# First involution of a four-layer convolution network: which engine's queue issues the fourth copy of shifted patches

## The chip, the cores and the metric

The kernel runs on one core of one Trainium2 chip, in one launch. The metric is the device time of the whole program in microseconds (us). The kernel before took 1796.4 us, the median of three runs (1794.46 to 1797.01).

A core has five engines that run side by side, each with its own queue of instructions that it works off in order: PE (TensorE, matmuls), DVE (VectorE), ACT (ScalarE), POOL (GpSimd) and SP (SyncE, which here only issues transfers). A transfer (DMA) is issued by an instruction in the queue of SP, ACT or POOL and then runs on the core's DMA engines; its landing is told by a semaphore.

## The reference, cut to what matters

The input is x, 4 images of 256 channels of 56 x 56, all in float32. Four layers follow, each of which adds its result to x. Layers 0 and 2 are involutions, layer 1 is two 3x3 convolutions, layer 3 gates with Fourier transforms. The change touches layer 0 alone:

```python
x = x + _L0_conv_ref(_gn(x), ...)            # _gn: normalise groups of 8 channels

# _L0_conv_ref
patches = conv_general_dilated_patches(x, (7, 7), ...)      # the 49 neighbours of each pixel
patches = patches.reshape(b, G, c // G, 49, 56, 56)         # G = 16 groups of 16 channels
h = einsum('bchw,oc->bohw', x, reduce_w) + reduce_b         # 256 -> 64 channels
kern = einsum('bchw,oc->bohw', h, span_w) + span_b          # 64 -> 49 taps for each group
kern = kern.reshape(b, G, 1, 49, 56, 56)
out = (kern * patches).sum(axis=3)
```

Every pixel and group of channels has its own 7 x 7 filter, computed from the normalised input.

## The kernel before, in words

**Units and columns.** `involution_layer` works on 8 units, one for each image and each block of 128 channels. An image is cut into tiles of 3 rows by 8 columns of pixels (TY, TX); a tile needs a window of 9 x 14 = 126 pixels around it (QY, QX, Q). Seven tiles side by side make the width, so a unit has 7 columns (NTX) of 19 tiles each (NTY). There are 56 columns in the layer, numbered here from 0.

**First phase of a unit, the taps.** `tap_matrices` computes for every tile a matrix `kt` that holds the filters laid out over the window's 126 pixels. It is made of matmuls of `z_sb` with `hp` (L593), whose results DVE (L611) and ACT (L604) copy out with the bias.

**Second phase, the columns.** For each of the 7 columns the loop calls `apply`, `next_windows` and `next_strip`, in this order. `apply` multiplies the column's windows `xw` with `kt` (L635, 112 matmuls), ACT and DVE pick the right groups out of the products into `un` (L648, L655), and POOL adds them to x (L660).

**How a column's windows come about.** `next_strip` lets POOL write a normalised strip of the image, 14 pixels wide, into `strip_sb` (L391), of which there is one. `next_windows` has TensorE transpose it in seven pieces (L406), and ACT copies these into `xw` (L418). The seven pieces are the windows of every third tile, those that start on a multiple of 9 rows. The windows in between start 3 or 6 rows lower, and are put together from two neighbours: for a shift of j = 1 or 2 times 3 rows, one copy takes the lower part of a window, `xw[cut:Q]`, and one the upper part of the window after it, `xw[:cut]`, where `cut` is 42 j pixels. So there are four copies a column, all within `xw`, of 84, 42, 42 and 84 partitions with 3 KB each: 252, 126, 126 and 252 KB. The first of each pair is issued at L424, the second at L426.

**What sets the order.** `xw` has three buffers (NXW), so `next_windows` in column c makes the windows of column c + 3. For the last three columns of a unit these are the first three of the next, which are used only after that unit's taps. At a unit's start the transposes for the first call come before column 0 is applied; in the other calls they come after the column's `apply`. `in_order` keeps each engine's instructions in the order in which the program writes them. The scheduling layer adds the waits: a copy waits for ACT's L418, and the first use of `xw` in L635 waits for all four copies. SP's transfers take turns among eight semaphores, and each waits until the transfer that last used its semaphore has landed.

**What else is in these queues.** SP loads a new image's blocks at L294, in the middle of the taps. POOL also computes a power for the normalisation (L149), and stores a finished unit (L1120) after its last strip. In the last unit ACT's queue issues loads of the next layer's weights.

In layer 2 the same function runs with all four copies issued by SP; its strips are written by ACT (L389) from the third column on.

Of the kernel before, what the change touches and what calls it, by code (L numbers as in the profile page):

```python
# [35 lines left out]
Q = QY * QX  # L36
# [35 lines left out]
def net_kernel(  # L72
# [19 lines left out]
    nc = tc.nc  # L92
# [206 lines left out]
    def involution_layer(layer, xin, xout, red, span, sb, xs_of, ahead=None, pending=None):  # L299

        with ExitStack() as es:
# [91 lines left out]
            def window(ty):  # L393

                k, j = divmod(ty, TY)
                return (0, NSB, 2 * NSB - 1)[j] + k
# [3 lines left out]
            def begin_windows():  # L400

                flat = strips[len(xws)].rearrange("p h w -> p (h w)")
                ps = two_banks().rearrange("p i n -> p (i n)")
                begun_windows.append(ps)
                for k in range(NSB):
                    nc.tensor.transpose(ps[:Q, k * P : (k + 1) * P], flat[:, k * Q : (k + 1) * Q], ident_sb)  # L406

            def next_windows():

                if len(xws) == len(columns):  # L410
                    return
                if not begun_windows:
                    begin_windows()
                ps = begun_windows.pop()
                xw = work.tile([Q, NTY, P], F32, name="xw", bufs=NXW)
                xws.append(xw)

                nc.scalar.copy(xw[:, :NSB, :], ps[:Q, : NSB * P].rearrange("q (n c) -> q n c", n=NSB))  # L418

                n = NSB - 1  # L420
                for j in range(1, TY):
                    cut = TY * QX * j
                    at = window(j)
                    nc.sync.dma_start(xw[: Q - cut, at : at + n, :], xw[cut:Q, 0:n, :])  # L424
                    eng = nc.sync if layer == 2 or j == 1 else nc.gpsimd
                    eng.dma_start(xw[Q - cut : Q, at : at + n, :], xw[:cut, 1 : 1 + n, :])  # L426


            h_of = {}
# [537 lines left out]
            if layer == 0:  # L967
                place(hooks0, begin(), (1, 2, 4, 6, 7))
            else:
                since = mark()  # L970
                nc.sync.dma_start(z_sb, z2_dram)
                nc.sync.dma_start(zb_sb, zb2_dram)
                next_strip()
                run(bottleneck(0))
                hooks0[3] = list(pending[0])
                for _ in range(NXW - 1):
                    next_windows()
                    next_strip()
                hooks0[7] = [next_windows, next_strip]
            if layer == 0:  # L980
                next_strip()
                for i in range(NXW):
                    hooks0.setdefault(2 + 5 * i, []).extend((next_windows, next_strip))
# [34 lines left out]
            for u, (b, cb) in enumerate(units):  # L1018
# [24 lines left out]
                if b + 1 < B:  # L1043
                    n = 16 if layer == 0 else (26, 21)[cb]
# [714 lines left out]
```

## Time and profile before

The profiled execution is one run of the program.

| what | value |
|---|---|
| median of three runs | 1796.4 us (1794.46 to 1797.01) |
| profiled execution, first to last instruction (the page gives no other time of its own) | 1791.4 us |
| difference between the two | 5.0 us |
| first involution, layer 0 | from the start to about 513 us |
| TensorE busy, whole span | 1716.7 us (96%) |
| DVE, ACT, POOL busy | 1385.3, 813.5, 406.2 us |
| POOL's issue of the fourth copy, L426 | 56 times, 31.5 us in all, mean 563 ns |
| SP's issues of window copies between 0 and 520 us | 168 times, medians 786 (L424) and 767 ns (L426) |

In a row of the costliest groups the first part names line, engine, operation and tiles (out<-in, with partitions x elements); after the count stand busy time and the mean of one in ns, and after the second bar the idle time of the engine just ahead of such instructions, with what ended it. In the chain of waits each line has start, duration and what ran; "issue" is time in which the profile shows nothing to wait for. For waits the three numbers are the total, the number of times and the longest.

### The profile page before, as it was taken

The page shows a single profiled execution, that of the slowest core. Times are in us where ns is not written, and L with a number is a line of the kernel's source. Part 1 is how long each engine was busy: PE and PEld are TensorE (multiplying, and loading weights), DVE is VectorE, ACT ScalarE, POOL GpSimd, SP SyncE. Part 2 cuts the span into 40 slices and gives each one's busy share as a digit, 9 for nine tenths or more (in the row PEclk, how much of TensorE's full clock was granted, in tenths as well). Part 3 has the DMA queues.
Part 4 walks back from the last instruction along what each step waited for, and adds up shares of the span by engine and source line. Part 5 has one row for each costly group of instructions (what it writes and reads, how often), then busy time and mean ns, then how long its engine had stood idle before and what let it go on. Part 6 is the DMA issues. An engine that isn't in the chain of part 4 may idle for free.

```text
span 1791.4 us, 55774 instructions
## 1 busy us (share of the span) xinstructions
PE 1716.7 (96%) x24040; PEld 1507.5 (84%) x24040; DVE 1385.3 (77%) x2745; ACT 813.5 (45%) x1882; POOL 406.2 (23%) x627
## 2 busy tenths in 40 slices
PE   6999999999999999999999999999999999999998
PEld 4998988889978988898889888986888887788886
DVE  2777787767778988988898889885777778687775
ACT  2555556555533222222323132111767667567564
POOL 2224422444320000000000000001000355463572
PEclk9999999999989999999999999999999999999997
DMA  2445444633653021211111111122344567566653
GB/s 86 135 151 170 140 146 134 196 107 119 204 171 105 32 75 51 76 33 64 58 68 44 52 63 37 44 110 73 122 164 156 162 213 220 169 223 189 183 154 115
DMA packets 66003, 215.76 MB, mean 120 GB/s; under 512 B 13237, under 2 KB 20926, under 8 KB 62046
## 3 DMA queue, kind: packets, MB, share of 16 engines
q1 hardware_dynamic: 49262, 145.37, 25.9%
q0 software_dynamic: 14656, 64.77, 11.3%
q8 instruction: 190, 3.11, 0.7%
q10 hardware_dynamic: 1840, 2.05, 0.4%
q14 instruction: 55, 0.45, 0.1%
HBM read 76.30 MB, written 49.15 MB: 70 GB/s over the span
## 4 chain that ended last, share of the span: by engine, by line
PE 68%; DVE 19%; ACT 4%; DMA 4%; issue 3%; POOL 2%; SPq 1%; POOLq 0%; ACTq 0%; DVEq 0%
PE mm L1523 17%; PE ps L593 14%; PE ps L635 14%; PE mm L1441 9%; DVE kt L611 6%; PE mm L1412 5%; PE ps L406 3%; DMA xw<-xw 3%; DVE un L655 3%; PE ps L469 1%; DVE res L1516 1%; DVE xs L1375 1%; DVE st L1105 1%; ACT kt L604 1%; ACT hp L488 1%
## 5 line engine op out<-in xcount | busy, mean ns | idle before, releaser
L635 PE MATMUL ps<-kt,xw 126*32 126x48 f32 (+1 forms) x12544 | 381.8, 235 | 27.8 <-issue 12.2
L635 PEld LDWEIGHTS ps<-kt,xw 126*32 126x32 f32 (+1 forms) x12544 | 341.9, 121 | 74.5 <-issue 45.5
L593 PE MATMUL ps<-hp,z_sb 64*126 64x133 f32 x6144 | 383.2, 279 | 8.4 <-DVE kt L611 4.6
L1523 PE MATMUL mm<-v,u_sb 128*128 128x280 f32 (+1 forms) x1728 | 383.5, 383 | 1.9 <-DVE u_sb L1254 1.5
L593 PEld LDWEIGHTS ps<-hp,z_sb 64*126 64x126 f32 x6144 | 363.6, 185 | 24.4 <-DVE kt L611 6.8
L611 DVE TENSOR_TENSOR kt<-ps,zb_sb 126x798 f32<-126x798 f32 x352 | 332.9, 980 | 60.4 <-PE ps L593 49.2
L1523 PEld LDWEIGHTS mm<-v,u_sb 128*128 128x128 f32 x1728 | 326.1, 189 | 56.3 <-DVE u_sb L1254 1.9
L604 ACT ACTIVATE kt<-ps,zb_sb 126x133 f32<-126x133 f32 x960 | 280.1, 441 | 107.3 <-PE ps L593 107.3
L1441 PE MATMUL mm<-v,u_sb 128*128 128x252 f32 (+1 forms) x936 | 209.5, 384 | 0.0
L1441 PEld LDWEIGHTS mm<-v,u_sb 128*128 128x128 f32 x936 | 176.4, 189 | 30.5 <-issue 0.8
L655 DVE SCALAR_TENSOR_TENSOR un<-ps,s,un 128x240 f32<-128x240 f32 x224 | 102.6, 458 | 86.7 <-ACT un L650 79.9
L1560 POOL DMA_DIRECT2D x<-xs x24 | 13.1, 547 | 680.1 <-DVE xs L1559 426.5
L655 DVE SCALAR_TENSOR_TENSOR un<-ps,par_sb,un 128x240 f32<-128x240 f32 x224 | 98.1, 457 | 86.8 <-ACT un L648 82.3
L1508 ACT ACTIVATE res<-xs,shift,norm_sb 128x1120 f32<-128x1120 f32 (+1 forms) x24 | 30.2, 1258 | 236.3 <-DVE xs L1559 107.3
L418 ACT COPY xw<-ps 126x896 f32<-126x896 f32 x112 | 101.2, 905 | 44.0 <-PE ps L406 38.5
L406 PE MATMUL ps<-ident_sb,strip_sb 128*126 128x128 f32 x784 | 111.9, 283 | 8.4 <-POOL strip_sb L391 5.3
L660 POOL TENSOR_TENSOR xs<-un,xs 128x240 f32<-128x240 f32 x112 | 72.1, 664 | 192.2 <-DVE un L655 192.1
L648 ACT ACTIVATE un<-ps,par_sb 128x240 f32<-128x240 f32 x112 | 50.1, 448 | 122.5 <-PE ps L635 120.6
L650 ACT ACTIVATE un<-ps,bn_t,s 128x240 f32<-128x240 f32 x112 | 60.1, 537 | 94.7 <-PE ps L635 88.7
L406 PEld LDWEIGHTS ps<-ident_sb,strip_sb 128*126 128x126 f32 x784 | 85.1, 142 | 19.5 <-POOL strip_sb L391 8.3
L1412 PE MATMUL mm<-xs,u_sb 128*128 128x126 f32 (+1 forms) x792 | 98.7, 277 | 2.3 <-DVE xs L1375 1.3
L1412 PEld LDWEIGHTS mm<-xs,u_sb 128*128 128x128 f32 x792 | 94.4, 191 | 3.7 <-DVE xs L1428 1.6
(256 smaller groups left out, 1903.1 us busy)
## 6 DMA issues: line engine op xcount, KB each, us to landing
xw<-xw SPq DMA_DIRECT2D x168, 252.0 KB
xw<-xw SPq DMA_DIRECT2D x224, 126.0 KB
xw<-xw POOLq DMA_DIRECT2D x56, 252.0 KB, 4.6
xs<-x SPq DMA_DIRECT2D x24, 560.0 KB
x<-xs POOLq DMA_DIRECT2D x8, 1568.0 KB, 7.5
xs<-x SPq DMA_DIRECT2D x8, 1568.0 KB
xs<-in_x_dram SPq DMA_DIRECT2D x6, 1568.0 KB
x<-xs SPq DMA_DIRECT2D x6, 1568.0 KB
```

The costliest lines, as they stand in the source:

```text
L406: nc.tensor.transpose(ps[:Q, k * P : (k + 1) * P], flat[:, k * Q : (k + 1) * Q], ident_sb)
L418: nc.scalar.copy(xw[:, :NSB, :], ps[:Q, : NSB * P].rearrange("q (n c) -> q n c", n=NSB))
L593: nc.tensor.matmul(ps[:Q, i, k * NT : (k + 1) * NT], z_sb[i * R : (i + 1) * R, cb * GB // 2 + gp, z0 : z0 + Q], hp[i * R : (i + 1) * R, py ...
L604: nc.scalar.activation(kt[:, g0 + i, pb, :, k], ps[:Q, i, k * NT : (k + 1) * NT], AF.Identity, bias=zb_sb[:, cb * GB + g0 + i, p0 + k : p0 ...
L611: nc.vector.tensor_tensor(kt[:, g0 : g0 + 2, pb], ps[:Q, :, : PB * NT].rearrange("q i (k t) -> q i t k", k=PB), zb_sb[:, cb * GB + g0 : cb ...
L635: nc.tensor.matmul(v[m * j : m * j + m, i, :, k * TP : (k + 1) * TP], xw[:, window(ty), m * j : m * j + m], kt[:, ng * j : ng * j + ng, :, ...
L650: nc.scalar.activation(part, o[0], AF.Identity, bias=bn["t4"][:, cb : cb + 1], scale=bn["s4"][ng][:, 0, cb : cb + 1])
L655: nc.vector.scalar_tensor_tensor(part, o[e], s, part, ALU.mult, ALU.add)
L660: nc.gpsimd.tensor_tensor(dst, u, dst, ALU.add)
L1412: nc.tensor.matmul(ps[:, co * m : (co + 1) * m], u[ci][:, co * P : (co + 1) * P], v2[:, e, : n // 2, ci * WT : (ci + 1) * WT], start=(ci = ...
L1441: nc.tensor.matmul(ps, u1_sb[:, ci, dy, k, co * P : (co + 1) * P], v[:, k, dy * NB + ci : (dy + n - 1) * NB + ci + 1 : NB, :], start=(j == 0),
L1523: nc.tensor.matmul(ps, u2_sb[:, ci, dy, k, co * P : (co + 1) * P], v[:, k, dy * NB + ci : (dy + n - 1) * NB + ci + 1 : NB, :], start=(j == 0),
```

## The change

For layer 0 and j = 2 the second copy, of 84 partitions from `xw[:84]` to `xw[42:126]`, is issued by SP instead of POOL. It thereby comes fourth in SP's queue for each column, after the other three. The copy itself, its bytes and what waits for it stay as they are. Layer 2 is as before.

```diff
                     nc.sync.dma_start(xw[: Q - cut, at : at + n, :], xw[cut:Q, 0:n, :])
-                    eng = nc.sync if layer == 2 or j == 1 else nc.gpsimd
-                    eng.dma_start(xw[Q - cut : Q, at : at + n, :], xw[:cut, 1 : 1 + n, :])
+                    nc.sync.dma_start(xw[Q - cut : Q, at : at + n, :], xw[:cut, 1 : 1 + n, :])
```

From this place on the lines of the kernel after have numbers that are lower by one.

## Prediction

> **What bounds the kernel now.** I read the page first, then the waits and the chain of the first involution alone (0 to 520 us of the span of 1791.4 us), then each window copy on its own. TensorE is busy in 96% of the span, so only what leaves a gap on TensorE counts. Two rows of the page carry most of the stage, and two rows name the queues concerned:
>
> ```profile
> L635 PE MATMUL ps<-kt,xw 126*32 126x48 f32 (+1 forms) x12544 | 381.8, 235 | 27.8 <-issue 12.2
> L406 PE MATMUL ps<-ident_sb,strip_sb 128*126 128x128 f32 x784 | 111.9, 283 | 8.4 <-POOL strip_sb L391 5.3
> ...
> xw<-xw SPq DMA_DIRECT2D x224, 126.0 KB
> xw<-xw POOLq DMA_DIRECT2D x56, 252.0 KB, 4.6
> ```
>
> The last row is what moves: 56 copies of 252 KB, one a column. The reader is to see that L406, the transposes, have 8.4 us of idle time ahead of them, 5.3 of it ended by POOL's L391. The waits between 0 and 520 us say how often (total, times, longest):
>
> ```profile
> POOL xw L426 <- ACT xw L418: 26.9, 13, 16.2
> ...
> PE ps L406 <- POOL strip_sb L391: 5.3, 8, 0.8
> ...
> PE ps L635 <- DMA xw<-xw: 2.8, 3, 1.3
> PEld ps L635 <- DMA xw<-xw: 2.5, 2, 1.5
> ```
>
> Eight times is once in each of the eight units (image and channel block). TensorE's waits for window copies, 2.8 + 2.5 = 5.3 us, all lie in the last unit: the same query between 488 and 513 us gives the same 5.3. The chain of waits in the third unit shows where the moved DMA stands (start, us, what):
>
> ```profile
> 195.56 0.32 POOL xs L660
> ...
> 196.22 0.63 POOL xs L660
> 196.85 0.52 POOL xw L426
> 197.37 0.05 issue
> 197.41 1.01 POOL strip_sb L391
> 198.42 0.04 issue
> 198.46 0.98 PE ps L406 x7
> ```
>
> So **POOL's issue of the fourth copy is itself on the chain**, 0.52 us between the residual add L660 and the strip L391 for which TensorE stands idle (0.79 us here). The chain looks the same at 78.5, 135.3, 252.7, 315.0, 371.7, 434.0 and 488.1 us. In the second unit it passes L426 once more, at 147.79 us, on to L391, the power L149 and a normalised weight (L232).
>
> **What the Trainium skill says.** "DMA: Bandwidth & Descriptors", section "Issuing engines are not separate DMA queues": all queues run on the same 16 engines, and several issuers save only sequencer time, usually small. The trace agrees on the kind, but here it is not small: an SP issue takes 0.76 to 1.95 us (median 0.78), a POOL issue 0.55, against a column of 4.12 us. The table in the section "Latency and other measured facts" gives a first byte after about 0.6 us for SP's path and 1 us for POOL's. The trace shows no clear gain for SP: from issue to landing POOL's copies take at least 3.4 us (median 4.6), and SP's first copy, in quiet columns, 3.3 to 3.6. Section "Queues, rings and completion order": an engine goes round its queues packet by packet. So where ACT's queue also has work, one window queue instead of two has a smaller turn; no row of before shows that alone.
>
> **The change part by part.**
>
> *1. POOL loses 56 DMA issues.* 56 x 0.563 us = 31.5 us of busy time (the row of L426 on POOL). POOL is idle most of the stage, so all but the places on the chain is worth nothing: it is hidden under TensorE's L635. On the chain it is worth the start of L391 moving from 197.41 to the end of L660 (196.85) plus 0.04 us of issue: 0.52 us. The gaps ahead of L406 in the eight units are 0.67, 0.55, 0.79, 0.78, 0.77, 0.43, 0.59 and 0.77 us; each can give at most itself, so 7 x 0.52 + 0.43 = 4.1 us. The second unit's pass over L149 gives another 0.5: **4.6 us gained**. The bounds are 0 (another wait takes over; in the third unit, L660's own lateness leaves 0.27 of the 0.79) and 5.9 (5.35 for all the gaps, 0.5 more). POOL's wait for ACT's L418 (26.9 us, 13 times) goes too; what queues behind it, strips and adds, has time in other columns. The stores of x behind the last strip start half a microsecond earlier, in a tap phase, where nobody waits for them.
>
> *2. SP gains 56 issues, each after the three others.* SP's three begin 0.03, 0.86 and 1.67 us after the ACT copy. The fourth can begin at 2.49 instead of POOL's 0.3 to 1.0. SP's work per column becomes 4 x 0.82 = 3.3 us of 4.12, if no issue stretches. Queued behind it are the next column's first copy, with 0.8 us to spare, and the loads of x, issued in a tap phase some 30 us before anything uses them: nothing. An eighth-last SP copy must have landed before a semaphore is used again; this is now two columns ago instead of 2.7, about 8.2 us, and the first copy lands within 5 to 6. I cost it at nothing; the cover is gone if a landing takes over 8.
>
> *3. The fourth copy lands later.* When a copy lands is in the trace's semaphore increments: the last of the four now comes 5.3 to 7.6 us after the ACT copy (mean 6.4) in the four late columns of the first seven units. Columns 0 to 2 of a unit have over 20 us; the four others are used in the same unit. Columns 17 to 20 (third unit) are applied 7.68, 7.19, 7.16 and 7.23 us after their ACT copy, with 0.97, 1.26, 1.00 and 0.44 us to spare; 45 to 48 (seventh unit) have 1.30, 0.73, 1.15 and 0.38, and the fifth unit 1.46, 1.41, 0.79 and 1.32. The other units are looser: 1.2 to 2.3 in the first, over 5 in half the columns of those with a bottleneck. An earlier strip brings the first of the four 0.5 us closer; the later three move along with TensorE.
>
> The operation is not in this stage's rows, but the second involution has it: it issues all four on SP. In its first two units, ahead of the gate's traffic, the fourth lands 5.8 to 8.0 us after the ACT copy (mean of eleven: 6.8), with no SP issue over 1.3 us. That is my value, some 0.5 later than today. Over the limit of about 7.2 were two of eleven, by 0.8 and 0.3. The expected worst of the three columns before the turn is about 0.27, the fourth adds 0.11 (a stall moves the next copies along, so it is not paid three times). For the three tight units: 3 x 0.38 = 1.1 us. The four loose ones: 0.2 together.
>
> The last unit is different: ACT's weight loads fill the DMA engines (share 0.84 between 488 and 500 us, against 0.67 at 200 to 216), landings come at 7.5, 9.8, 10.6 and 8.7 us. In crowded columns of the second involution the fourth lands about 0.9 after the third. So the wait, now 5.3 in all, grows by about 1.0 (0 to 3). **2.3 us lost**; bounds 0 (the copies no longer meet POOL's stream, and the end stays) and 11 (8.5 us landings in every tight column, 6.5, the last unit 3, the looser ones 1.5).
>
> **The sum.** -4.6 + 2.3 = -2.3 us: the profiled execution from 1791.4 to 1789.1, and the median of the three runs, which is 5.0 us above that span, from 1796.4 to **1794.1**. About 0.2% (3.6 us) is what a measurement of this kernel can tell from no change, so I call this no change with a lean to faster.
>
> **Rivals.**
>
> *A queue on SP replaces the queue on POOL (slower).* The fourth is last in one in-order queue; a stretched issue (1.95 us has occurred) pushes it past 3.3 us, the next column starts late, and landings come at 8 to 8.5. At 8.0 the deficits are 1.6 us in each of two tight units, 0.9 in the fifth, 1.3 in the looser, 3 in the last: 8.4, less 4.6, gives +3.8: 1800. At 8.5: +6, 1802. It decides from a landing some 1.3 us later than today's last one on, where losses exceed 4.6. For it: in the second involution TensorE waits 13.5 us for window copies against 5.3 here. Against: most of that is under gate traffic, and the stretched issues in the first involution come where POOL's stream runs beside SP's.
>
> *The transfer is hidden anyway (faster).* The bytes are the same, and without POOL's copy SP's own third may land earlier, at 4.7 to 5 as in quiet columns of the second involution. Then only part 1 is left: -4.6, 1791.8. Against: the four margins under 0.8 us.
>
> *It does not do what it says.* If POOL's place on the chain is taken by L660 or by TensorE's next wait, and the copies are in time, nothing is left: 1796.4, within the middle case.
>
> **How the numbers follow.** Middle case, both effects of like size: 0.45. Slower by over 3.6 us, the SP queue: 0.29. Faster by over 3.6 us: 0.26. The range 1790.0 to 1802.0 takes in the faster rival and the slower one at 8.5 us, and leaves out the full 5.9 us gain and the worst of the last unit.
>
> **What would show it.** Right: the waits of L406 for L391 fall from 5.3 to under 1.5 us; L426's successor on SP begins at about 2.5 us; TensorE's waits for window copies rise from 5.3 to 7 to 8 us. Wrong: waits for copies over 10 us, or in many units, give the SP queue; a wait of L406 that stays at 5 us says that POOL's issue was not what held the strip.

## The result, and the profile after

The kernel after took 1791.2 us (median of nine runs, 1784.36 to 1798.22) against 1797.01 us for the kernel before on the same chip: a ratio of 0.9969, interval 0.9955 to 0.9984, so 2.9 to 8.1 us less. Timed again later it was 0.9961 (0.9949 to 0.9974). The change makes the kernel faster by about 6 us, in the forecast's direction and inside its range, but by more than twice the 2.3 us that it named: what came is the case of "faster by over 3.6 us", which it held at 0.26. The profiled execution of after spans 1788.9 us against 1791.4, only 2.5 us less; single executions scatter too much to read such a change from spans, as the experiments show.

From the page of the kernel after, the rows of what moved and of the transposes (columns as before):

```profile
L406 PE MATMUL ps<-ident_sb,strip_sb 128*126 128x128 f32 x784 | 111.0, 282 | 5.3 <-issue 1.7
...
xw<-xw SPq DMA_DIRECT2D x224, 252.0 KB
xw<-xw SPq DMA_DIRECT2D x224, 126.0 KB
```

All 448 window copies of both involutions are now on SP, and L406's idle time fell from 8.4 to 5.3 us. Who ends the waits in the first involution (0 to 520 us; total, times, longest):

```profile
DVE norm_sb L232 <- POOL norm_sb L149: 7.3, 7, 1.7
...
PE ps L634 <- issue: 2.2, 3, 1.0
...
PE ps L406 <- POOL strip_sb L391: 1.2, 6, 0.2
...
PE ps L634 <- DMA xw<-xw: 0.8, 3, 0.3
```

TensorE's waits for strips are down from 5.3 to 1.2 us, and DVE's wait for the power L149 from 9.7 to 7.3; its line of before is:

```profile
DVE norm_sb L232 <- POOL norm_sb L149: 9.7, 7, 2.4
```

The matmuls' waits for window copies did not grow: 2.8 us before, 0.8 after. The chain of waits at the third unit's start, the place quoted of before (start, us, what):

```profile
196.48 0.32 POOL xs L659
196.81 0.34 issue
197.14 0.64 POOL xs L659
197.78 1.00 POOL strip_sb L391
198.78 0.04 issue
198.82 1.00 PE ps L406 x7
```

The strip now follows the residual add without a gap. From the first add's start to the transposes it takes 2.34 us; it was 2.90.

Where the time came from is best read by **column phases**, from a unit's first application matmul to its last. The eight together take 255.8 us before and 249.7 after. The seven taps phases between them are alike to half a microsecond in total. The rest of the program moved both ways: before the first column phase +1.7 us, between the last column and the second involution's first +1.5, the second involution's columns -1.9. The change does not touch those parts. The +1.5 lies ahead of the convolutions' first matmul (13.8 us after the last column before, 15.3 after; 14.0 and 15.7 in a second pair of profiles), and over all kernels below this stretch scatters from 12.1 to 15.8.

### The profile page after: what moved, and what is told of

It reads as the page before. It is cut to its first block, busy times and chain, and to the rows that moved or that the text cites. A ratio compares the mean times of both kernels' runs of the same rounds, so it can differ in the third digit from the quotient of the medians.

```text
span 1788.9 us, 55629 instructions
## 1 busy us (share of the span) xinstructions
PE 1719.6 (96%) x24040; PEld 1510.4 (84%) x24040; DVE 1385.5 (77%) x2745; ACT 814.5 (46%) x1882; POOL 377.3 (21%) x571
## 3 DMA queue, kind: packets, MB, share of 16 engines
q1 hardware_dynamic: 54750, 159.83, 28.4%
## 4 chain that ended last, share of the span: by engine, by line
PE 68%; DVE 18%; DMA 4%; issue 4%; ACT 3%; POOL 1%; SPq 1%; ACTq 0%; DVEq 0%; POOLq 0%
PE mm L1522 17%; PE ps L592 14%; PE ps L634 13%; PE mm L1440 10%; DVE kt L610 5%; PE mm L1411 5%; DMA xw<-xw 4%; PE ps L406 3%; DVE un L654 3%; PE ps L468 2%; DVE res L1515 1%; DVE xs L1374 1%; DVE st L1104 1%; ACT hp L487 1%; PE ps L717 1%
## 5 line engine op out<-in xcount | busy, mean ns | idle before, releaser
L659 POOL TENSOR_TENSOR xs<-un,xs 128x240 f32<-128x240 f32 x112 | 72.2, 666 | 218.6 <-DVE un L654 218.6
L406 PE MATMUL ps<-ident_sb,strip_sb 128*126 128x128 f32 x784 | 111.0, 282 | 5.3 <-issue 1.7
L406 PEld LDWEIGHTS ps<-ident_sb,strip_sb 128*126 128x126 f32 x784 | 84.3, 141 | 16.5 <-POOL strip_sb L391 4.2
```

The costliest lines, as they stand in the source:

```text
L659: nc.gpsimd.tensor_tensor(dst, u, dst, ALU.add)
```

## The experiments

All ratios are to the kernel before, timed on the same chip. Times in column phases come from one profile of each kernel. The last unit scatters most (28.4 to 33.7 us over all kernels), so the first seven are summed alone as well.

**The kernel before once more.** No edit. 

> The kernel before once more, for the scatter of one profile. The sum of the eight column phases (first to last application matmul of a unit) was 255.8 us in the first profile of before and 249.7 after. If that difference is the change's, this profile gives 254 to 257 again, with waits of L406 for the strip L391 near 5.3 us; if it is scatter of single executions, anywhere from 249 to 257. Time: ratio 0.998 to 1.002.

Ratio 1.0003 (0.999 to 1.0016). Column phases 255.0 us. The first seven units took 225.1 and 225.5 us in the two profiles; the second, third, fourth, sixth and seventh agree to 0.1 us each. So the phases are a sharper measure than the span, which was 1793.2 here, 1.8 longer. The matmuls' waits for window copies at L635, 2.8 us in the first profile, were 0.8 here: that figure was one execution's.

**The kernel after once more.** No edit. 

> The kernel after once more. If the change is worth 5 us or more: ratio 0.995 to 0.998 and column phases of 249 to 251 us. If the profile's sum of 2.3 us was right and the rest is scatter: ratio 0.998 to 1.0 and column phases of 252 to 254 us.

Ratio 0.9961. Column phases 249.9 us. The gain of 5 to 6 us in this stage is the change's, not scatter. Single units differ by up to 0.9 us between the two profiles of after, the sum of the first seven by 0.8 (220.0 and 220.8).

**Only a unit's first column on SP.**

```diff
-                    eng = nc.sync if layer == 2 or j == 1 else nc.gpsimd
+                    first = len(xws) % NTX == 4
+                    eng = nc.sync if layer == 2 or j == 1 or first else nc.gpsimd
```

> Only the fourth copy that is issued in the first column of a unit, 8 of 56, goes to SP; the other 48 stay on POOL. Theory A (POOL's issue ahead of the strip at a unit's start is what counted): the waits of L406 for L391 fall to under 2 us as with the whole change, column phases fall by 4 to 5 us against before, ratio about 0.9975. Theory B (the gain comes from the other columns, where POOL's stream no longer runs beside SP's): waits fall, but column phases fall by no more than 1 to 2 us and the ratio is 0.999 to 1.0.

Ratio 0.9989 (0.9978 to 1.0001). TensorE's waits for strips fell to 1.7 us, and the first seven units took 222.4 us, 2.9 less than before; with the whole change it is 4.9 less. By the profile the strip at a unit's start is thus a good half of the gain, by the timing (2.0 us of 5.6 to 7.0) about a third. Neither expectation was met in full: all eight phases together came to 256.1 us, no less than before, because the last unit took 33.7 us. Of that, 3.7 was one gap of a kind that is described below.

**The complement: that column alone on POOL.** The same edit with `not first`. 

> The complement: 48 fourth copies go to SP, the 8 issued in a unit's first column stay on POOL. Theory A: waits of L406 for L391 stay at about 5 us, column phases change by -1 to +2 us against before, ratio 0.9995 to 1.001. Theory B: waits stay, yet column phases fall by 3 to 5 us, ratio about 0.998.

Ratio 0.9969 (0.9957 to 0.9981). The strips are waited for as before (6.4 us), yet the first seven units took 222.5 us, also 2.8 less; all eight together fell by 2.0, less than theory B asked for. So the 48 other issues count as much in the profile, and in the timing they make nearly the whole gain. The prediction had costed all but one of them at nothing.

**The copies on SP, and POOL kept busy instead.**

```diff
+            if layer == 0:
+                pad = wpool.tile([P, 560], F32, name="pad")
...
                     nc.sync.dma_start(xw[Q - cut : Q, at : at + n, :], xw[:cut, 1 : 1 + n, :])
+                if layer == 0:
+                    nc.gpsimd.memset(pad, 0.0)
```

> The kernel after, with a memset of 560 elements on a spare tile (about 0.55 us, as long as the DMA issue was) in POOL's queue at the place of the moved issue, in layer 0. The output is unchanged. Theory A (the time that POOL spends on the issue, ahead of the strip L391 and of the power L149, is what the change took off the chain): the gain is lost, waits of L406 for L391 back at 4.5 to 6 us, column phases of the first involution 253 to 256 us (before 255 to 256, after 249.7 and 249.9), ratio 0.999 to 1.0005. Theory B (two window streams, one from each kind of queue, slow each other's copies): column phases stay at 249 to 251 us, ratio 0.996 to 0.9975.

Ratio 0.9993 (0.998 to 1.0006): the gain is gone. L406 is L408 in this kernel. The group of the filler (busy time, mean ns of one) and the wait for strips between 0 and 520 us:

```profile
L429 POOL MEMSET pad<- 128x560 f32 x56 | 31.7, 567 | 0.0
```

```profile
PE ps L408 <- POOL strip_sb L391: 5.4, 8, 0.7
```

As many instructions as there were issues, and as long (567 against 563 ns), bring back the old wait to a tenth of a microsecond, with the transfers still on SP. So **what POOL spends on issuing is most of what the change took off the path**, not the way the bytes go. Column phases were 254.2 us, just under before (255.0 and 255.8); the first seven units took 223.7, which is two thirds of the way back. The filler slowed no other group that was compared: DVE's operations into `un` take 457 ns each with it and 456 without, TensorE's matmuls with the windows 235.4 and 234.5 ns.

**The filler in a unit's first column alone.** The memset is issued only where `len(xws) % NTX == 4`. 

> The kernel after with the 0.57 us memset on POOL in 8 of 56 columns alone, those where the window copies are made in a unit's first column. The output is unchanged. It splits Theory A into its two places. Waits of L406 for L391 come back to about 5 us in 8 places, those of L468 and of L232 for L149 stay as after (L232 about 7.3 us). If the strip at a unit's start is the larger part: column phases of the first seven units 222.5 to 224 us (after 220.0 and 220.8, before 225.1 and 225.5). If the path over L149 is: 220.5 to 222. Ratio 0.9965 to 0.999.

Ratio 0.9983 (0.997 to 0.9995). Waits for strips 5.0 us in eight places, L232's wait for L149 7.9, the first seven units 220.0 us, as after. Column phases did not show the loss; the timed ratio does, with 2.5 to 4.0 us lost against the kernel after, though the intervals overlap. What restoring the strip's delay alone costs is therefore not settled.

**The issue behind the strip, still on POOL.**

```diff
+            def issue_fourth():
+                while fourth:
+                    nc.gpsimd.dma_start(*fourth.pop())
...
-                    eng = nc.sync if layer == 2 or j == 1 else nc.gpsimd
-                    eng.dma_start(xw[Q - cut : Q, at : at + n, :], xw[:cut, 1 : 1 + n, :])
+                    if layer == 2 or j == 1:
+                        nc.sync.dma_start(xw[Q - cut : Q, at : at + n, :], xw[:cut, 1 : 1 + n, :])
+                    else:
+                        fourth.append((xw[Q - cut : Q, at : at + n, :], xw[:cut, 1 : 1 + n, :]))
```

`next_strip` calls `issue_fourth` at its end. 

> The kernel before, but POOL issues the fourth copy after the next strip L391 instead of before it. Theory A: the strips come 0.55 us sooner, waits of L406 for L391 fall to 1 to 2 us; the power L149 still queues behind the issue, and the fourth copy is issued about 1.5 us later than before; column phases 251 to 254 us, ratio 0.9975 to 0.999. Theory B: nothing of the two streams changes, column phases 254 to 257 us, ratio 0.9995 to 1.001.

Waits for strips 1.0 us, as with the whole change, but the ratio was 0.9993 (0.9975 to 1.001), and L232's wait for L149 stayed at 9.6 us. Column phases were 254.2 us. Both figures miss theory A's ranges by a little: freeing the strips was worth less than it asked for (first seven units 223.1 us, 2.2 less than before).

**The strip before the first application.** The fourth copy stays on POOL.

```diff
+                    if layer == 0 and tx == 0:
+                        next_strip()
                     apply(b, cb, kt, tx, xws[u * NTX + tx])
                     next_windows()
-                    next_strip()
+                    if not (layer == 0 and tx == 0):
+                        next_strip()
```

> The kernel before, with the first strip of a unit's column phase written ahead of the first application instead of behind it (layer 0), so that neither the issue nor the residual add stands ahead of it; the fourth copy stays on POOL. Theory A, the strip's part of it: waits of L406 for L391 near 0 at unit starts, column phases of the first seven units 221.5 to 223.5 us, ratio 0.9975 to 0.999, with the path over L149 still as before (L232 waits 9 to 10 us). Were the two streams the cause: 224 to 226 us, ratio 0.9995 to 1.0005.

The waits for strips are nearly gone (0.9 us, in two places), but nothing is gained: ratio 1.0005 (0.9992 to 1.0018), first seven units 225.6 us. That is where the expectation had put the two streams as the cause, and it is the instructive miss. Against the mean of the two profiles of before, the three units with a bottleneck (second, fourth and sixth) took 1.5 us less, the four others 1.8 more. In the third unit SP's three copies landed 8.2 us after the ACT copy in one column whose application began after 7.2; TensorE stood still for 0.57 us there. Most of the rest went into gaps that no engine's work ended. The chain of waits of this kernel in the third unit:

```profile
217.07 2.37 PE ps L635 x44
219.44 1.22 issue
220.66 1.14 PE ps L635 x54
```

In the middle of 112 like matmuls, with all their data there, TensorE stands still for 1.22 us. The same was in the kernel before, in the fourth unit:

```profile
266.90 0.55 PE ps L635 x26
267.44 0.61 issue
268.05 0.80 PE ps L635 x42
```

Counted along TensorE's instructions, such gaps stand at multiples of 256 from each other (9409 and 9665 in the fourth unit, 12738 in the fifth, with a miss of one). In the column phases of all 14 profiles TensorE has 79 gaps of over 0.1 us that the profile gives to "issue", and 77 of them stand at these marks (two, of under 0.2 us, fall together with a late copy in column 47). The other 75 end 2.2 to 3.1 us (median 2.5) after the last packet of 16,384 bytes of the kind "instruction" started on the DMA engines. They look like waits for TensorE's next instructions. That is inferred; no run took the fetches away.

**Twice the suspected cost.** Both copies of j = 2 are issued by POOL in layer 0.

```diff
-                    nc.sync.dma_start(xw[: Q - cut, at : at + n, :], xw[cut:Q, 0:n, :])
                     eng = nc.sync if layer == 2 or j == 1 else nc.gpsimd
+                    eng.dma_start(xw[: Q - cut, at : at + n, :], xw[cut:Q, 0:n, :])
```

> The kernel before with both copies of the second pair (j = 2) on POOL: the suspected cost twice. Theory A: another 0.55 us per unit start and before each L149: waits of L406 for L391 about 10 us, column phases 259 to 262 us, ratio 1.002 to 1.003. Theory B: only 126 KB more a column in POOL's stream, waits 5 to 7 us and column phases 255 to 258 us, or longer waits for window copies at L635 instead of for strips.

Ratio 1.0071 (1.005 to 1.0092), 12.7 us slower, and column phases of 268.2 us: more than twice the expected loss. The waits for strips between 0 and 520 us:

```profile
PE ps L406 <- POOL strip_sb L391: 14.8, 27, 1.3
```

Not 8 places but 27: with 1.1 us of issuing in each column POOL falls behind in later columns too. Where between one and two issues this begins was not measured.

**The two large copies first on SP.** The four copies are gathered in a list and issued in the order 0, 3, 1, 2 in layer 0. 

> The kernel after, with the two copies of 252 KB issued first and the two of 126 KB last, in layer 0. If the late fourth copy still costs something after the change (it landed up to 0.8 us too late in three columns), the last landing comes 0.3 to 0.6 us sooner and column phases fall to 248.5 to 249.5 us, L634's waits for window copies near 0 outside the last unit; ratio to before 0.9955 to 0.9965. If landings no longer bound anything: 249.5 to 250.5 us and the ratio of the kernel after, 0.9961 to 0.9969.

Ratio 0.9971 (0.9959 to 0.9983), no better than after. The last landing stayed at 6.6 us on average in the late columns, so a smaller last copy did not land sooner. Waits for window copies were 2.8 us, nearly all in the last unit. Column phases were 250.8 us, of which the first seven units took 218.6, a little less than after; the timing shows nothing of it.

**Early strip and SP together.** The early strip's edit on the kernel after. 

> Both: the fourth copy on SP and the early strip (layer 0). Waits of L406 for L391 fall from 1.0 to 1.2 us to under 0.4; the first windows of a unit are then 0.2 us tighter. Column phases of the first seven units 219 to 220.5 us; ratio to before 0.9955 to 0.9968, at most 0.1% better than the kernel after.

Ratio 0.9964 (0.9948 to 0.9979). No wait for a strip is left in the list, and the first seven units took 217.0 us, 3 to 4 less than after, better than expected. The last unit gave some back, with 3.1 us of waiting for one window copy. The time is that of the kernel after, within its interval, and the next run shows how far the 217.0 can be trusted.

**The early strip in both involutions.** The condition is `tx == 0` alone. 

> The same with the early strip in the second involution too, where ACT writes it. There TensorE's waits at unit starts are not for strips, and ACT's residue of taps stands ahead: no gain expected over the run with layer 0 alone, ratio 0.9955 to 0.9975; a loss if ACT's strip delays the first un.

Ratio 0.9962 (0.995 to 0.9975): no further gain, as expected. In the first involution this kernel is the same as the one before it, yet its first seven units took 219.2 us against 217.0. So one profile's figure for them can be off by some 2 us, and smaller differences between kernels are not to be read from it.

**The account.** From each profile the gaps of over 0.1 us at the 256-instruction marks that the profile gives to "issue" can be taken out of the first seven column phases:

| kernel | waits L406 for strip, us | first seven, us | gaps at the marks | rest | ratio |
|---|---|---|---|---|---|
| before (two profiles) | 5.3, 6.1 | 225.1, 225.5 | 3.1, 3.3 | 222.0, 222.2 | 1, 1.0003 |
| after (two profiles) | 1.2, 1.0 | 220.0, 220.8 | 1.9, 2.8 | 218.1, 218.0 | 0.9969, 0.9961 |
| first column on SP | 1.7 | 222.4 | 3.3 | 219.1 | 0.9989 |
| others on SP | 6.4 | 222.5 | 1.2 | 221.2 | 0.9969 |
| SP, filler everywhere | 5.4 | 223.7 | 2.0 | 221.7 | 0.9993 |
| SP, filler in first column | 5.0 | 220.0 | 0.7 | 219.3 | 0.9983 |
| POOL, issue behind strip | 1.0 | 223.1 | 3.5 | 219.6 | 0.9993 |
| POOL, early strip | 0.9 | 225.6 | 6.3 | 219.3 | 1.0005 |
| two on POOL | 14.8 | 237.8 | 6.1 | 231.6 | 1.0071 |
| SP, the large copies first | 1.0 | 218.6 | 1.4 | 217.3 | 0.9971 |
| SP, early strip | none listed | 217.0 | 1.0 | 216.0 | 0.9964 |
| SP, early strip in both involutions | none listed | 219.2 | 2.1 | 217.1 | 0.9962 |

The column "rest" falls by 4.0 us from before to after, and the filler brings all but 0.4 back: that is POOL's issue time. From before, three of the four come with the first columns (219.1) and nearly one with the others (221.2). From after, the filler in the first columns puts back only 1.2 (219.3), so the parts do not simply add. The gaps at the marks are 3.1 to 6.3 us in the kernels with at least 48 copies in POOL's stream and 0.7 to 2.8 us in those with 8 or none. From before to after they fall by about 1 us, and in the run with the others on SP they are 2.0 of the 2.8 us gained.

## Why the prediction was right, and where it was off

**Part 1, POOL's issue on the path: right in the place and near in the sum.** It named L426 between the add and the strip, up to 0.52 us in each of eight units, 4.1 us in all. The waits fell from 5.3 and 6.1 us to 1.2 and 1.0, by 4.1 and 5.1; that the issue's duration makes these waits, the filler shows. With the 0.5 for L149 it came to 4.6 us, and "rest" fell by 4.0. How the 4.0 divide is less clear: the three kernels that free the strips and leave POOL's stream (first column on SP, issue behind the strip, early strip) gain 2.5 to 3.0 us of "rest", but 2.0, 1.3 and -0.9 us in the timing. The path over L149 was seen in the second unit only. It is there in the sixth too: the waits ahead of the matmuls of L469 fell from 0.81 to 0.21 us in the second unit and from 0.78 to nothing in the sixth, and the second pair of profiles shows the same.

**Part 2, SP's queue: right.** The fourth copy begins at 2.49 us or a little later. SP needs 0.78 us an issue, and 28 of 224 issues took over 0.95 us; before it was 47 of 168. The slower rival, an SP queue that stretches and falls behind, did not come about: with POOL's stream gone SP's issues stretch less, as that rival's own "against" had said. (Its bound of 6.5 us for landings at 8.5 comes to 7.2 by the sum that it used at 8.0.)

**Part 3, the later landing: the term was too large.** It gave 0.5 us; the mean of the last landing in the 28 late columns rose from 6.35 us (6.39 in the second profile) to 6.61 (6.53), by 0.2. SP's first three copies, which have no copy of POOL's beside them, have landed after 5.3 instead of 6.35 us, and the fourth follows 1.3 later. The limit was also set too early. The description of the kernel before has the first use of `xw` in L635 wait for all four copies, and the prediction measured its margins to a column's first matmul. The trace shows otherwise: a column begins with a tile whose window ACT wrote, and waits for the third and fourth copy only some tenths of a microsecond later. In column 18 the fourth copy landed 0.8 us after the column's first matmul; TensorE ran eight matmuls in 0.61 us and then stood still for 0.31. In column 47 it landed 0.5 us after, and TensorE stood still for 0.13. The second profile of after has 0.31 us in column 18 again and no other gap of over 0.1 us for a copy in the first seven units. The term had 1.3 us; at most 0.4 was lost.

**The last unit: the added microsecond is not seen.** The prediction added 1.0 us to a wait of 5.3 us, on the ground that ACT's weight loads leave one window queue a smaller turn. The 5.3 was a wrong sum: the 2.5 us are idle time of TensorE's weight loads, and they lie in the same stalls as the matmuls' 2.8 (499.02 to 500.54 us and 499.24 to 500.55, for one). TensorE stood still for 2.8 us, and the 13.5 us quoted for the second involution are about 9 in the same way. The wait was no property of the kernel either. It is 2.8 and 0.8 us in the two profiles of before, 0.8 and 2.8 in those of after, and the unit took 30.7 and 29.5 us before, 29.6 and 29.0 after. The rise to 7 to 8 us that it gave as a sign of being right did not come, and no run supports the smaller turn. The step that failed was to read a single execution as typical in the one unit that scatters.

**A term was missing.** Gaps on TensorE that the profile gives to "issue" were left out of the sum as if they were fixed. They shrink by about 1 us when POOL's stream is gone. In the sum, 4.0 us of "rest", 0.9 of gaps and 0.8 in the last unit, which scatters by more than that, make the 5.6 us by which the column phases fell, and the timed 5.6 to 7.0 us agree with it. The faster rival was the closest: it named 1791.8 us. Its reason was half of the truth, for the later landing was nearly hidden. That its figure fits so well is in part luck, because the gaps make up for what part 1 had too much.

**What stays open.** How much the 8 issues in the first columns are worth and how much the 48 others. The complement (48 on SP) gained 3.4 to 7.7 us in the timing, but only 2.0 us in its profile's column phases; by the timing the others make nearly all of the gain, by "rest" a quarter. Whether single profiles or the timing, which also takes in the scatter of the other layers, are the better witness isn't settled. Nor is it shown why the gaps at the marks are longer with POOL's stream.

## What to carry to other kernels

An issue that costs half a microsecond is not free on an engine that also computes: look in the chain of waits for the issuing instruction itself, and ask what stands behind it in that queue. Against the transfer, which takes 4.6 us from issue to landing, the issue is small; against the strip that stood behind it in POOL's queue it was not. Removing one wait by moving work forward can be worth nothing when late copies and gaps take its place (the early strip with the copies on POOL). Idle times of TensorE's matmuls and of its weight loads are not to be added, since both can show one stall. Before a wait is taken for a cost to build on, look at it in a second execution.

## What the runs showed of the hardware that was not expected

TensorE stopped for 0.1 to 3.7 us at places 256 instructions apart, where the profile shows nothing to wait for, some 2.5 us after a packet of 16,384 bytes of the kind "instruction" started. With 48 or more window copies in POOL's stream this cost 3.1 to 6.3 us over seven units, with 8 or none 0.7 to 2.8.

SP's copies landed later while POOL's was under way: the first of them in the late columns landed 4.7 us after the ACT copy before, and 3.9 us after the change. For that first copy it is the time at which POOL's copy is issued that counts, not that there are two streams. With the issue behind the strip, about 1.4 us after the ACT copy, SP's first copy landed at 3.9 us too, and its third at 6.4, as before. The fourth copy's landing moved by only 0.2 us, although it is issued some 2 us later.

The first-byte times that the prediction cites do not come out here, as far as the first packet can stand for the first byte: POOL's path was not the slower one. In the trace of before, where the queue had been still, the first packet on SP's queue started at least 1.43 us after the issue of a column's first copy began (median 1.47), and on POOL's queue at least 1.12 us after (median 1.37).
